# Values as the loaded operand of the value product in the second local-attention model

## The chip, the cores and the metric

The kernel runs on one core of one Trainium2 chip. The metric is the device time of one execution in microseconds (us). The engines of the core run side by side, each in the order of its own instruction list, and wait for each other through semaphores: TensorE (PE in the profile; its weight loads are shown apart as PEld), VectorE (DVE), ScalarE (ACT), GpSimd (POOL) and SyncE (SP), which here issues the DMAs.

## What is computed

Two blocks follow each other on a tensor of 2 sequences of 2048 tokens with 128 features. Each block is an adaptive layer norm around an attention part and a feed-forward part, and in each block the "feed-forward part" is itself a small transformer with local attention. The first of these (below: the first model) has 6 layers, 16 heads of 64 and windows of 32 tokens; the second has 2 layers, 8 heads of 64 and windows of 64 tokens. The change lies in the attention of the second one. For each head, each window of 64 queries looks at the 128 keys of its own window and the one before:

```
sim  = einsum('bhwid,bhwjd->bhwij', bq, bk)      # masked
attn = softmax(sim, -1)
out  = einsum('bhwij,bhwjd->bhwid', attn, bv)    # the value product
o    = out.transpose(0, 2, 1, 3).reshape(b, n, INNER)
x    = x + o @ wo
```

All of it is in float32.

## The kernel before, in words

The program has three stages. The first attention part takes a little over 600 us (the first value product of L1047 starts at 624 us). Then comes the first local model, and from about 4040 us to the end the second one. The linear attention that stands between the two models is cut in small steps ("lsteps") and woven in between the tiles of both.

A local model is worked off in tiles of 128 tokens. A layer has 16 tiles for each of the 2 sequences, so that the second model has 2 x 16 x 2 = 64 tiles. The main loop of `local_models` (L1484 on) writes several tiles in flight into one turn: the scores of tile i + 1, the projections of tile i + 3 (`project`), the values and the turning of queries and keys of tile i + 2 (`values`, `turn`), and the value product and output of tile i. A scheduling layer then settles the order on each engine, and puts one tile's work into the gaps of another's. The order in which the engines run is fixed when the program is built.

What a tile of the second model goes through, with its lines:

- `project` (L862): queries and keys from one matmul pair into PSUM (L871); squares on ACT (L873); rotary products on DVE (L881, L886); their sum on POOL (L892); norms on DVE (L897 and the small steps of `rsqrt_quick`, L167 to L180); the scaling on POOL (L904), whose result is the tile `r`.
- `turn` (L923): eight transposes of `r` on PE (L936) and two copies on ACT (L939, L941) give queries and keys with features on the partitions.
- `values` (L943): one matmul (L955), a copy on ACT (L956), and DMAs (L965 to L968) that lay out the 128 keys of each window on the partitions, in the tile `v2`, two tiles ahead of its use.
- `scores` (L974): the mask is written by a matmul (L986), and 16 matmuls of 64 x 64 x 128 add the scores (L995). Then come maximum (L1003) and difference (L1005) on DVE, the exponential on ACT (L1012), sum and reciprocal on DVE (L1019, L1020) and the scaling on POOL (L1021).
- `keys_first_` (L1023): eight transposes (L1030) and two copies on ACT (L1031) put the keys on the partitions, in the tile `pT`.
- `mix` (L1034): the value product. For each of 8 heads and 2 windows one matmul loads a 128 keys x 64 queries part of `pT` and streams the 128 keys x 64 features of `v2` through it (L1047), so that 64 queries lie on the partitions of the result. One copy on ACT (L1053) brings the PSUM bank to the tile `on`.
- `turn_out` (L1056): four transposes on PE (L1063) and a copy on ACT (L1064) turn `on` into `oT`, with features on the partitions.
- `project_out` (L1067): four matmuls with the output weights (L1075) and two additions on DVE (L1081).

Every fourth tile of a sequence a feed-forward step of that sequence's 512 tokens is queued (L1144 on) and worked off in the following turns; its hidden products are L1158, its Gelu on ACT L1168, its second product L1183. Exponential and Gelu need different tables on ACT, and each change between them costs an ACT_TABLE_LOAD, which the profile lists under the line of the activation that follows it.

PSUM banks for these steps come in turn from a pool of four (`bank`), so each new bank waits until the one four requests back has been read. `pT` and `oT` share one SBUF buffer; `on` has one of its own. `m.NO` is 128 / (2 x window): 2 in the first model, 1 in the second.

Of the kernel before, what the change touches and what calls it, by code (L numbers as in the profile page):

```python
# [72 lines left out]
def tile_kernel(ctx: ExitStack, tc: tile.TileContext, a: dict, out: bass.AP):  # L73
    nc = tc.nc
# [633 lines left out]
    def local_models(mA, mB, hs0):  # L708
# [12 lines left out]
        def bank(name):  # L721
            return psT.tile([128, 512], F32, tag="T", name=f"ps_{name}")
# [53 lines left out]
        st = [dict() for _ in range(n)]  # L776
# [4 lines left out]
        def load_proj(g, u):  # L781

            m, l = layers[g]
            w = wpool.tile([128, 1024], F32, tag="wp", name="wp", bufs=4)
            c = u * 1024
            k = min(1024, 3 * m.INNER - c)
            nc.sync.dma_start(w[:, 0:k], a[f"{m.pre}_ffn_Wqkv"][l, :, c:c + k])
            wts[g, u] = w

        def load_out(g):  # L790
            m, l = layers[g]
            w = wpool.tile([128, 8, 128], F32, tag="wo", name="wo", bufs=2)
            nc.sync.dma_start(
                w[:, 0:m.NPR, :], a[f"{m.pre}_ffn_Wo"][l].rearrange("(c p) m -> p c m", p=128)
            )
            wts[g, "o"] = w
# [41 lines left out]
        def factors(g):  # L838
            m, l = layers[g]
            f = wk.tile([128, 2, 2, DH], F32, name="fac", bufs=2)  # L840
            nc.vector.scalar_tensor_tensor(
                f[:, 0], m.sc, RSQ_C, m.qsc[:, :, l, :], ALU.mult, ALU.mult
            )
            for lo in (0, 32):
                nc.vector.tensor_copy(f[:, 1, :, lo:lo + 32], f[:, 0, :, 32 - lo:64 - lo])
            fac[g] = f
# [127 lines left out]
        def scores(i):  # L974

            g, b, t = tiles[i]
            m, _ = layers[g]
            W, H, HPG = m.W, m.H, m.HPG
            qT, kT = st[i].pop("q"), st[i].pop("k")
            sp = wide("s")  # L980
            for q in range(2):


                rows, sel, j = (slice(0, 128), identb, 0) if t == 0 else (
                    slice(64 * q, 64 * q + 64), pick, 1)
                nc.tensor.matmul(  # L986
                    sp[:, 512 * q:512 * q + 512], lhsT=sel[rows],
                    rhs=bc(m.maskb[rows, j].unsqueeze(1), (rows.stop - rows.start, HPG, 2 * W)),
                    start=True, stop=False,
                )  # L990
            for cc in range(HPG):
                for q in range(2):
                    for w in range(m.NW):
                        c0 = 512 * q + 2 * W * cc
                        nc.tensor.matmul(  # L995
                            sp[W * w:W * w + W, c0:c0 + 2 * W],
                            lhsT=qT[64 * q:64 * q + 64, cc, W * w:W * w + W],
                            rhs=kT[64 * q:64 * q + 64, cc, W * w:W * w + 2 * W],
                            start=False, stop=(cc == HPG - 1),
                        )  # L1000
            v = lambda x: x.rearrange("p (h k) -> p h k", k=2 * W)
            mx = wk.tile([128, 16], F32, name="mx")
            nc.vector.tensor_reduce(mx[:, 0:H], v(sp), AX.X, ALU.max)  # L1003
            sm = wk.tile([128, 1024], F32, name="sm", bufs=2)
            nc.vector.tensor_tensor(  # L1005
                v(sm), v(sp), bc(mx[:, 0:H].unsqueeze(2), (128, H, 2 * W)), ALU.subtract
            )
            st[i]["p"] = sm

        def weights_exp(i):  # L1010
            sm = st[i]["p"]
            nc.scalar.activation(sm, sm, AF.Exp)  # L1012

        def weights_norm(i):
            m, _ = layers[tiles[i][0]]
            sm = st[i]["p"]
            v = sm.rearrange("p (h k) -> p h k", k=2 * m.W)
            rs = wk.tile([128, 16], F32, name="rs", bufs=2)[:, 0:m.H]
            nc.vector.tensor_reduce(rs, v, AX.X, ALU.add)  # L1019
            nc.vector.reciprocal(rs, rs)  # L1020
            nc.gpsimd.tensor_tensor(v, v, bc(rs.unsqueeze(2), (128, m.H, 2 * m.W)), ALU.mult)  # L1021
# [12 lines left out]
        def mix(i):  # L1034

            m, _ = layers[tiles[i][0]]
            W, NO = m.W, m.NO
            pT, v2 = st[i].pop("pT"), st[i].pop("v")
            po = [bank("o") for _ in range(NO)]
            on = wk.tile([128, 2, 4, 128], F32, name="on")  # L1040
            for c in range(4):
                for s in range(NO):
                    kp = slice(2 * W * s, 2 * W * (s + 1))
                    for q in range(2):
                        co = 128 * c + 64 * q
                        for w in range(m.NW):
                            nc.tensor.matmul(  # L1047
                                po[s][W * w:W * w + W, co:co + 64],
                                lhsT=pT[kp, q, c, W * w:W * w + W],
                                rhs=v2[kp, w, co:co + 64], start=True, stop=True,  # L1050
                            )
            for s in range(NO):
                nc.scalar.copy(on[:, s].rearrange("p c i -> p (c i)"), po[s])  # L1053
            st[i]["on"] = on
# [34 lines left out]
        def step():  # L1089
            if steps:  # L1090
                steps.pop(0)()
# [4 lines left out]
        def lstep():  # L1096
            if lsteps:
                lsteps.pop(0)()
# [372 lines left out]
        for i in range(-3, n):  # L1471
            j = i + 3
            lstep()
            if 0 <= i + 1 < n:
                scores(i + 1)
                weights_exp(i + 1)
                weights_norm(i + 1)
            more = False
            if j < n:
                g, b, t = tiles[j]  # L1480
                jj = j % per
                nu = len(layers[g][0].units)
                more = g < last
                if g == second and t % 4 == 0:  # L1484
                    while (b, t // 4) not in ready:
                        lstep()
                if nu == 2:
                    project(j, 0)
                if more and jj == 4:
                    load_proj(g + 1, 0)  # L1490
                if more and jj == 6 and g + 1 == second:
                    models[1].consts()
                if jj == 6 and g == second - 1:
                    linear_consts()
                if more and jj == 8:
                    factors(g + 1)
                    if 2 == 2:
                        load_out(g + 1)
                if more and jj == 18:
                    load_ff(g + 1)  # L1500
                if more and jj == 22:
                    fold_ff(g + 1)
                if nu == 2 and more and jj == per - 1:
                    load_proj(g + 1, 1)
                lstep()
            step()
            if i >= 0:
                keys_first_(i)
            if 0 <= i + 2 < n:
                halo(i + 2)  # L1510
            if j < n:
                project(j, nu - 1)
                if nu == 2 and more and jj == per - 1 and g + 1 < second:
                    load_proj(g + 1, 2)
                if nu == 1 and more and jj == per - 1:
                    load_proj(g + 1, 1)
                if b == B - 1 and j + 1 < n:
                    tables(*tiles[j + 1][::2])
            lstep()
            if i >= 0:  # L1520
                mix(i)
            lstep()
            if 0 <= i + 2 < n:
                values(i + 2)
            lstep()
            if i >= 0:
                turn_out(i)
            if 0 <= i + 2 < n:
                for u in range(len(layers[tiles[i + 2][0]][0].units)):
                    turn(i + 2, u)  # L1530
            step()
            lstep()
            if i >= 0:
                g, b, t = tiles[i]
                project_out(i)
                if 2 == 1 and i % per == per - 1 and g < last:
                    load_out(g + 1)
                if t % 4 == 3:
                    feed_forward(g, b, t // 4)
# [9 lines left out]
    with ExitStack() as ctx2:  # L1549
        local_models(m0, m1, hs0)  # L1550
# [63 lines left out]
```

## Time and profile before

| | |
|---|---|
| median of 3 runs | 5001.14 us (4997.42 to 5006.03) |
| profiled execution, its own time | 5004.26 us |
| its span | 5002.5 us |
| mean granted TensorE clock | 0.961 of full |

Busy time in the stretch of the second model, 4043 us to the end (960 us), from the view of busy time by stretch:

| engine | busy us | share |
|---|---|---|
| PE | 846.9 | 88% |
| DVE | 721.8 | 75% |
| ACT | 544.1 | 57% |
| POOL | 442.1 | 46% |

A row of the groups view names the line, the engine and operation, the tiles written and read, shapes and count; then the busy time in us and the mean of one in ns; then the time for which the engine had stood idle just ahead of these instructions, and which work ended that. A matmul in float32 appears as two records, a transpose as one. The chain of waits is followed back from the last instruction: each piece has its start, the time it adds to the end, and the work. Matmul ends are modelled, so that four pipelined transposes show 0.66 us though their starts are only about 0.11 us apart.

### The profile page before, as it was taken

To read this page: it belongs to the slowest core of one execution; us is meant where nothing else is said; L and a number is where in the kernel's file an instruction comes from. 1 tells how busy PE (TensorE), PEld (TensorE's weight loads), DVE (VectorE), ACT (ScalarE), POOL (GpSimd) and SP (SyncE) were. 2 spreads that over 40 slices of the span, in tenths; PEclk is the share of its full clock that TensorE was granted. 3 is DMA by queue.
4 is the path that set the end of the run, shared out by engine and by line. 5 is a ranking of instruction groups with operands and counts; after the bars stand their busy time and mean duration, and the time that the engine had idled before them with its cause. 6 is when DMAs were issued, how large, how long until landed. Compare 5 with 4: busy or idle time off the path is not lost.

```text
span 5002.5 us, 170719 instructions
## 1 busy us (share of the span) xinstructions
PE 4572.7 (91%) x74820; PEld 3143.2 (63%) x74850; DVE 3973.1 (79%) x6840; ACT 2883.5 (58%) x4665; POOL 2780.8 (56%) x1666
## 2 busy tenths in 40 slices
PE   5667799999999999999999999999999989899897
PEld 4445566666666666666666666666666666555554
DVE  6993488888888888888888888888877777787885
ACT  3233366666666656666666666666555555565564
POOL 3332366666666666666666666666555544455452
PEclk8778899999999999999999999999999999999999
DMA  2000322222222322223222322232222211111111
GB/s 77 1 1 25 84 69 67 63 72 74 71 64 63 83 71 63 63 76 76 66 66 64 83 67 64 65 78 73 54 55 52 63 45 38 39 46 40 53 53 37
DMA packets 222487, 295.59 MB, mean 59 GB/s; under 512 B 75656, under 2 KB 95408, under 8 KB 221744
## 3 DMA queue, kind: packets, MB, share of 16 engines
q1 hardware_dynamic: 221744, 284.67, 22.0%
q8 instruction: 590, 9.67, 0.8%
q14 instruction: 153, 1.25, 0.1%
HBM read 40.98 MB, written 10.75 MB: 10 GB/s over the span
## 4 chain that ended last, share of the span: by engine, by line
PE 53%; DVE 20%; ACT 8%; POOL 5%; issue 3%; DMA 1%; SPq 0%; POOLq 0%; ACTq 0%; DVEq 0%
PE ps_qk L871 11%; PE ps_v L955 6%; PE ps_f L1158 5%; PE ps_turn L936 5%; PE ps_y L1075 5%; PE ps_o L1047 5%; PE ps_s L995 4%; DVE ps_qk L897 4%; POOL r L892 3%; DVE t L886 3%; PE ps_fy L1183 3%; PE ps_oT L1063 3%; ACT sq L873 2%; DVE r L881 2%; PE ps_pT L1030 2%
## 5 line engine op out<-in xcount | busy, mean ns | idle before, releaser
L892 POOL TENSOR_TENSOR r<-r,t 128x1024 f32<-128x1024 f32 x448 | 1061.2, 2369 | 995.9 <-DVE t L886 770.5
L904 POOL TENSOR_TENSOR r<-r,rq_y 128x1024 f32<-128x1024 f32 x448 | 844.0, 1902 | 455.9 <-DVE rq_y L180 439.2
L873 ACT ACTIVATE sq<-ps_qk 128x1024 f32<-128x1024 f32 x448 | 460.4, 1028 | 1006.4 <-PE ps_qk L871 999.9
L871 PE MATMUL ps_qk<-wp,hs 128*128 128x512 f32 x1792 | 884.4, 615 | 68.3 <-DVE rq_y L180 41.3
L881 DVE TENSOR_TENSOR r<-ps_qk,tb 128x1024 f32<-128x1024 f32 (+1 forms) x512 | 550.1, 1074 | 175.4 <-ACT sq L873 166.9
L886 DVE TENSOR_TENSOR t<-ps_qk,tb 128x1024 f32<-128x1024 f32 (+1 forms) x512 | 553.2, 1080 | 145.0 <-POOL r L892 144.5
L1021 POOL TENSOR_TENSOR sm<-sm,rs 128x1024 f32<-128x1024 f32 x256 | 487.2, 1903 | 263.3 <-DVE rs L1020 172.3
L897 DVE TENSOR_REDUCE ps_qk<-sq 128x16 f32<-128x1024 f32 x448 | 549.1, 1226 | 12.3
L1047 PEld LDWEIGHTS ps_o<-v,pT 64*32 64x32 f32 (+1 forms) x26624 | 356.8, 109 | 289.1 <-ACT pT L1031 175.7
L871 PEld LDWEIGHTS ps_qk<-wp,hs 128*128 128x128 f32 x1792 | 306.7, 191 | 326.2 <-issue 235.6
L955 PE MATMUL ps_v<-wp,hs 128*128 128x512 f32 x896 | 471.9, 639 | 1.0 <-ACT on L1053 0.6
L1047 PE MATMUL ps_o<-v,pT 64*32 64x64 f32 (+1 forms) x26624 | 418.1, 224 | 59.6 <-ACT pT L1031 32.7
L1075 PEld LDWEIGHTS ps_y<-oT,wo 128*128 128x128 f32 x3584 | 429.2, 192 | 48.0 <-issue 42.2
L936 PE MATMUL ps_turn<-ident,r 128*128 128x128 f32 x3584 | 443.2, 276 | 13.3 <-POOL r L904 11.8
L1075 PE MATMUL ps_y<-oT,wo 128*128 128x128 f32 x3584 | 446.3, 276 | 1.8 <-ACT oT L1064 1.8
L936 PEld LDWEIGHTS ps_turn<-ident,r 128*128 128x128 f32 x3584 | 405.7, 143 | 19.8 <-POOL r L904 16.6
L1003 DVE TENSOR_REDUCE mx<-ps_s 128x16 f32<-128x1024 f32 (+1 forms) x256 | 312.9, 1222 | 110.8 <-PE ps_s L995 107.4
L995 PE MATMUL ps_s<-kT,qT 64*32 64x64 f32 (+1 forms) x26624 | 371.6, 230 | 0.4
L1019 DVE TENSOR_REDUCE rs<-sm 128x16 f32<-128x1024 f32 (+1 forms) x256 | 310.3, 1212 | 68.6 <-ACT sm L1012 67.5
L1158 PE MATMUL ps_f<-fx,w 128*128 128x512 f32 (+1 forms) x768 | 356.4, 600 | 1.7 <-DVE fx L1141 1.7
L995 PEld LDWEIGHTS ps_s<-kT,qT 64*32 64x32 f32 (+1 forms) x26624 | 321.3, 107 | 57.1 <-issue 46.2
L956 ACT COPY vn<-ps_v 128x512 f32<-128x512 f32 x448 | 262.5, 586 | 112.3 <-PE ps_v L955 93.4
(268 smaller groups left out, 7554.6 us busy)
## 6 DMA issues: line engine op xcount, KB each, us to landing
v<-vn SPq DMA_DIRECT2D x1276, 128.0 KB
v<-vn SPq DMA_DIRECT2D x744, 64.0 KB
v<-vn SPq DMA_DIRECT2D x64, 256.0 KB
wp<-in_L_ffn_Wqkv SPq DMA_DIRECT2D x20, 512.0 KB
xD<-xb SPq DMA_DIRECT2D x24, 256.0 KB
xb<-xD SPq DMA_DIRECT2D x24, 256.0 KB
cs<-in_cos SPq DMA_DIRECT2D x128, 32.0 KB
cs<-in_sin SPq DMA_DIRECT2D x128, 32.0 KB
```

Of the source, the lines that this page charges most:

```text
L871: nc.tensor.matmul(pq[:, js], lhsT=hw, rhs=wts[g, u][:, js], start=True, stop=True)
L881: nc.vector.tensor_tensor(r[:, es].rearrange("p (h d) -> p h d", d=DH), pq[:, es].rearrange("p (h d) -> p h d", d=DH), bc(tb[:, 0, s].unsq ...
L886: nc.vector.tensor_tensor(t2[:, es].rearrange("p (h s d) -> p h s d", s=2, d=32), pq[:, es].rearrange("p (h s d) -> p h s d", s=2, d=32)[: ...
L892: nc.gpsimd.tensor_tensor(r, r, t2, ALU.add)
L897: nc.vector.tensor_reduce(pq[:, 16 * v:16 * v + 16], st[i].pop(("sq", v)).rearrange("p (h d) -> p h d", d=DH), AX.X, ALU.add,)
L904: nc.gpsimd.tensor_tensor(rv, rv, bc(y[:, 16 * v:16 * v + 16].unsqueeze(2), (128, 16, DH)), ALU.mult)
L936: nc.tensor.transpose(p[:, c * 128:(c + 1) * 128], r[:, cs], ident)
L955: nc.tensor.matmul(p, lhsT=hw, rhs=wv, start=True, stop=True)
L995: nc.tensor.matmul(sp[W * w:W * w + W, c0:c0 + 2 * W], lhsT=qT[64 * q:64 * q + 64, cc, W * w:W * w + W], rhs=kT[64 * q:64 * q + 64, cc, W ...
L1047: nc.tensor.matmul(po[s][W * w:W * w + W, co:co + 64], lhsT=pT[kp, q, c, W * w:W * w + W], rhs=v2[kp, w, co:co + 64], start=True, stop=True,)
L1075: nc.tensor.matmul(py[:, 0:128], lhsT=wts[g, "o"][:, c * NO + s, :], rhs=oT[:, s, c, :], start=(c + s == 0), stop=(c == 3 and s == NO - 1),)
L1158: nc.tensor.matmul(ps_[c][0:sz], lhsT=wts[g, "w1"][:, o:o + sz], rhs=S["x"], start=True, stop=True,)
```

## The change

In models with `NO == 1`, that is in the second one, the value product swaps its operands: the part of `v2` (128 keys x 64 features) is loaded and the part of `pT` (128 keys x 64 queries) is streamed. The result has the features of two heads on its 128 partitions and the queries along the free axis, as `oT` had. The copy on ACT brings it to `on`, and `project_out` reads `on` directly. `turn_out` isn't called for these tiles. The loop's innermost index is now the head of the pair (`q`), before it was the window (`w`). The first model keeps the old path.

```diff
             po = [bank("o") for _ in range(NO)]
             on = wk.tile([128, 2, 4, 128], F32, name="on")
+            if NO == 1:
+
+                for c in range(4):
+                    for w in range(m.NW):
+                        for q in range(2):
+                            co = 128 * c + 64 * q
+                            nc.tensor.matmul(
+                                po[0][64 * q:64 * q + 64, 128 * c + W * w:128 * c + W * w + W],
+                                lhsT=v2[:, w, co:co + 64], rhs=pT[:, q, c, W * w:W * w + W],
+                                start=True, stop=True,
+                            )
+                nc.scalar.copy(on[:, 0].rearrange("p c i -> p (c i)"), po[0])
+                st[i]["o"] = on
+                return
             for c in range(4):
                 for s in range(NO):
                     kp = slice(2 * W * s, 2 * W * (s + 1))
...
-            if i >= 0:
+            if i >= 0 and "on" in st[i]:
                 turn_out(i)
```

## Prediction

> **What bounds the kernel now.** I read the page's busy times and slices, then the busy time by stretch to find the second model, then groups and waits of that stretch (4043 us to the end), and last the chain of waits through it. On the page PE leads over the whole span:
>
> ```profile
> PE 4572.7 (91%) x74820; PEld 3143.2 (63%) x74850; DVE 3973.1 (79%) x6840; ACT 2883.5 (58%) x4665; POOL 2780.8 (56%) x1666
> ```
>
> The slices say that this holds for the first model (9 in each) but less for the last fifth, and only that part is changed. In it PE is busy 847 of 960 us, so 113 us are idle. The groups of that stretch, kept apart by form, and the waits of PE say where:
>
> ```profile
> L1047 PE MATMUL ps_o<-v,pT 128*64 128x64 f32 x2016 | 90.1, 236 | 23.2 <-ACT pT L1031 23.2
> L1063 PE MATMUL ps_oT<-ident,on 128*128 128x128 f32 x256 | 43.5, 295 | 27.8 <-ACT on L1053 27.3
> L1064 ACT COPY oT<-ps_oT 128x512 f32<-128x512 f32 x64 | 37.6, 588 | 39.5 <-PE ps_oT L1063 39.5
> PE ps_oT L1063 <- ACT on L1053: 27.3, 42, 2.0
> PE ps_turn L936 <- POOL r L904: 8.3, 8, 2.3
> ```
>
> The output transposes (L1063) are ahead of every other place in PE's waits: after the value product PE has to wait for ACT's copy before it can transpose. The chain shows that this is on the path, not only idle time. One tile near the end:
>
> ```profile
> 4889.90 1.72 PE ps_o L1047 x28
> 4891.62 0.02 issue
> 4891.64 0.59 ACT on L1053
> 4892.23 0.05 issue
> 4892.28 0.66 PE ps_oT L1063 x4
> 4892.94 0.87 PE ps_turn L936 x8
> 4893.81 2.58 PE ps_f L1158 x6
> 4896.39 0.90 PE ps_y L1075 x8
> ```
>
> The time between the value product and the turning of the next queries and keys is 0.02 + 0.59 + 0.05 + 0.66 = 1.32 us, in which PE does nothing but four transposes. The whole chain from 4040 us on runs through L1063 at 44 of the 64 tiles. But it is a mixed chain: between such places it goes over DVE (L1003, L1005), ACT (exponential and table loads) and POOL.
>
> **What is removed.** 64 tiles x 4 transposes on PE, 64 copies of 0.588 us on ACT (37.6 us), and PE's wait. From above, PE gets back at most busy plus wait, 43.5 + 27.8 = 71.3 us. That is too much for two reasons. Where PE had no wait, the transposes cost only the distance of their starts (about 0.44 us for four; 0.66 is the modelled end). And in some eight tiles the next work, the turn of L936, waits for POOL's r (8.3 us in all), so PE would only wait there instead.
>
> What is on the path I count on the chain: 44 steps of L1063 with 27.8 us, 36 steps of the copy to `on` (L1053) with 19.7 us, 6 of the copy to `oT` (L1064) with 3.5 us. That is **51 us**. The copy to `on` stays, but who waits for it changes: before, the transposes at once; after, the output product (L1075). PE does the turn first, 8 transposes of 0.87 us on the chain, against 0.05 + 0.59 us for the copy, so the new wait costs nothing where ACT is free. Where ACT is still at a square (1.02 us) when the product ends, the copy is late by that, and PE has the mask matmuls (L986, 2 x about 0.2) before the turn as well; I price it at nothing, at most 0.6 us in a tile. Without that cover the whole copy would be back on the path, 64 x 0.58 = 37 us. In the last two tiles there is no turn, and the copy stays visible; the transposes and their copy still go.
>
> **What is added.** Nothing in number: 16 matmuls before and after, each loading 128 x 64 and streaming 64 columns. The disputed price is that of the new form. The Trainium skill ("TensorEngine Tiling (Array Packing)", Performance Considerations) holds out up to twice the speed for swapping loaded and streamed operand together with column tiling where the streamed side is 64 or less. By that rule half of L1047's 90 us, 45 us, would come on top. The row says otherwise: the form before is 128*64 already, with an output of 64 partitions, so both halves of the array are taken before and after. I take the row: gain 0. The other bound is a loss. The output product streams 128 columns in about 0.13 us a record (8 in 1.05 us); 64 columns would be 0.065 us, yet 32 records of L1047 take 1.15 us in undisturbed tiles, 0.036 each. So two halves run side by side now. If they didn't after the swap, a product would cost 32 x 0.065 = 2.1 us, 0.95 more. Neighbouring matmuls still alternate between the halves (q inside, where it was w), so I take 0; the loss is kept for the rivals.
>
> The waits at the head of the product change places: `v2` is now loaded first, `pT` streamed. `v2` is written two tiles ahead, and no wait for its DMA shows among L1047's, so 0. The second matmul already needs the second copy of `pT`, before it was the third; the built order puts the values matmul (L955, about 1.05 us) in that gap as before, longer than the copy of 0.58. The `pT` buffer comes free earlier, since `oT` no longer sits in it, and `on` comes free at the output product, some 10 us before it is written again. A tile asks for one PSUM bank less, so each request looks back over other work; the banks it meets were read microseconds before. All these go at 0; a copy of 0.58 us in each tile (37 us) is the loss if I am wrong. SP's queue keeps its order but for five issues outside the attention.
>
> **What the scheduler moves.** The built order of the changed program has 148 table loads on ACT instead of 158: in five feed-forward steps the third Gelu now stands ahead of the exponential and not behind it. Each spares two loads:
>
> ```profile
> L1012 ACT ACT_TABLE_LOAD x26 | 33.4, 1283 | 39.9 <-DVE sm L1005 39.5
> L1168 ACT ACT_TABLE_LOAD x22 | 28.2, 1283 | 0.4
> ```
>
> The Trainium skill ("ScalarE: Activation LUTs", What ACT_TABLE_LOAD costs) states 1283 ns and about 1380 ns of drain, 2.66 us for a switch: ten would be 26.6 us. Here the chain has the exponential 0.01 us behind the load and the load 0.05 us behind its releaser; no drain is seen, so ten are 12.8 us of ACT. On the path I count less. In the chain at 4884 us an exponential ends at 4885.33, then load and Gelu follow, and the copy of `pT` that PE waits for starts at 4887.23: 1.9 us, of which the load is needed no more and the Gelu falls into ACT's earlier wait. 5 x 1.9 = **9.5 us**.
>
> **The sum.** 51 + 9.5 = 60 us from the path. Not all arrives: when PE is earlier, POOL's r and the copies of `pT` (23.2 us of PE's waits already) are late next, and DVE, busy 75% of the stretch, sets more of the pace. Much of that work starts from PE's own results (scores, projections) and moves up with it, so I take off a sixth: 50 us. The profiled execution, 5004.3 us (span 5002.5 and 1.8 around it), becomes 4954; the median lies 3.1 lower, so **4951 us**, 1.0% faster. A difference of 0.2% (10 us) is about what a measurement can tell.
>
> **Rivals.**
> 1. Likeliest (62%): as summed, 30 to 66 us less: 4935 to 4971.
> 2. The next wait takes half (20%): r (L904) and DVE's row of L1003, L1005, L1019 set the pace. For it: eight turns wait for r already, and the chain has long runs on DVE. Against it: DVE is idle a quarter of the stretch and its waits mostly end with PE or ACT. Gain 30 us or less: about 4973.
> 3. More than the path shows (11%): PE gets its 71 us nearly whole, as ACT also loses 37.6 + 12.8 = 50 us of work and the `pT` copies come earlier. For it: 23.2 us of waits for exactly these copies. Against it: the eight tiles bound by r. Gain 78 us: about 4923.
> 4. The swapped product is slower (4%): if the halves no longer overlap, 64 x 0.95 = 61 us are added at L1047, on the path behind which L1053 and L936 stand. Against the 50 us gained this gives 5012. It decides the sign from 0.8 us more a tile, that is, from about 1.95 us for an undisturbed product. Against it: same shape, same alternation.
> 5. It does nothing for the end (3%): the transposes were filler and DVE sets the pace throughout; 5001 within 10 us. Against it: 44 of 64 tiles on the chain.
>
> **How the numbers follow.** Faster by over 0.2% are cases 1 to 3, 0.93; within 0.2% is case 5, 0.03; slower is case 4, 0.04. The range leaves out the slow cases 4 and 5, the slower tail of case 2 and the far part of case 3: 4928 to 4977.
>
> **What would show it.** In the profile after, L1063 and L1064 keep only the first model's 1536 transposes and 384 copies. L1047's successor in the second model must stay near 90 us busy; over 120 would be case 4. The stretch of the second model should shrink from 960 to about 910 us with PE's share about unchanged or higher: 847 - 43.5 = 803 us of 910 is 88%. Waits of L936 for r should rise from 8.3, but stay under 25 us; well above that is case 2. Waits of L1075 for the copy to `on` should stay under 10 us. Table loads should count 148, and the first model's stretch should not change. I am wrong if the stretch shrinks by less than 30 us, or if the value product lengthens.

## The result: no change

The changed kernel takes 5001.44 us (median of 12 runs, 4997.21 to 5013.47), the kernel before in the same session 5001.52 us (12 runs, 4991.92 to 5008.41). The ratio is 0.9999, with a 95% interval of 0.9989 to 1.0008. The forecast was 4951 us. Its profiled execution took 5003.49 us, with a span of 5001.7 us, against 5004.26 and 5002.5 before; the mean granted TensorE clock was 0.956, against 0.961.

The swap did what the diff says. In the second model's stretch L1063 and L1064 are gone, the product still has 2016 recorded matmuls, and PE's wait for the copy to `on` has all but vanished. The groups of that stretch, by form (line and names; busy us and mean ns; idle before, and what ended it), after:

```profile
L1047 PE MATMUL ps_o<-pT,v 128*64 128x64 f32 x2016 | 93.4, 230 | 14.1 <-ACT pT L1031 14.0
L1172 PE MATMUL ps_f<-fx,w 128*128 128x512 f32 x144 | 81.5, 693 | 2.1 <-DVE fx L1155 1.8
L936 PE MATMUL ps_turn<-ident,r 128*128 128x128 f32 x496 | 75.7, 299 | 32.8 <-POOL r L904 32.8
```

And the waits of PE there, after (us in all, times, longest):

```profile
PE ps_turn L936 <- POOL r L904: 32.8, 11, 3.5
PE ps_o L1047 <- ACT pT L1031: 14.0, 33, 2.1
PE ps_out L1463 <- DVE xb L1219: 13.2, 4, 4.5
...
PE ps_y L1089 <- ACT on L1052: 1.5, 2, 0.7
```

The rows of before to set beside these (the value product, L1063 and two of the waits stand in the prediction):

```profile
L1158 PE MATMUL ps_f<-fx,w 128*128 128x512 f32 x144 | 72.8, 628 | 1.7 <-DVE fx L1141 1.7
L936 PE MATMUL ps_turn<-ident,r 128*128 128x128 f32 x496 | 69.6, 287 | 8.3 <-POOL r L904 8.3
PE ps_out L1449 <- DVE xb L1205: 4.7, 1, 4.7
```

The 27.3 us that PE waited for `on` are gone, and 9.2 us of its waits for `pT`. In their place the turn (L936) waits 32.8 us for POOL's `r`, where it waited 8.3, and the block output (now L1463) 13.2 us for DVE, where it waited 4.7. And some of PE's work got longer: the hidden products (L1158 before, L1172 now) had a mean of 628 ns and have 693, with the same shapes.

The sum of the busy times by stretch, 4043 us to the end, after:

```profile
sum 960.00, PE 837.68 PEld 536.20 DVE 714.49 ACT 498.53 POOL 443.64; mean PE 837.68 PEld 536.20 DVE 714.49 ACT 498.53 POOL 443.64
```

PE's busy time fell by only 9.2 us, from 846.9 to 837.7, and the stretch is 0.8 us shorter, so PE is idle 121 us in it and not 113. That gives an account of what PE was freed of. The row of L1063 says 43.5 us, but these records overlap with their neighbours: without them PE's busy time before would be 815.0 us, 31.9 less. With the waits for `on` and `pT` PE was thus freed of about 69 us. Of these 22.7 came back as longer times of the work that stayed (815.0 to 837.7), and 45 as new waits, over half of them for `r` (24.5).

The chain of waits shows how a tile comes to this. After, one tile in the middle of the stretch:

```profile
4702.42 0.18 DVE ps_qk L167
...
4702.63 1.23 DVE mx L1003
...
4703.97 1.23 DVE sm L1005
...
4705.30 1.06 ACT sm L1012
4706.36 0.02 issue
4706.38 1.22 DVE rs L1019
...
4708.01 0.17 POOL sm L1021
4708.18 1.69 issue
4709.87 1.91 POOL r L904
4711.78 0.04 issue
4711.82 1.28 PE ps_turn L936 x8
4713.10 4.08 PE ps_f L1172 x6
```

The norm's small steps (L167 to L180) run on DVE from 4702.42 to 4708.12, because one tile's maximum, difference and sum (L1003, L1005, L1019, about 1.2 us each) stand between the steps of another tile's norm. Then POOL scales that softmax first (L1021; the 0.17 and the 1.69 us of "issue" are its one instruction), and `r` after it, 1.6 us later than the norm would have let it start. PE stands still for 3.25 us ahead of the turn, so POOL's order is about half of this wait and DVE's the rest. The timeline of PE over the same place, after (start, length, work, and in brackets the wait ahead):

```profile
4711.82 1.28 PE L936 MATMUL ps_turn<-ident,r 128*128 128x128 f32 x8 [3.25 <-POOL r L904]
4712.90 4.29 PE L1172 MATMUL ps_f<-fx,w 128*128 128x512 f32 x6
...
4719.04 2.84 PE L1172 MATMUL ps_f<-fx,w 128*128 128x512 f32 x6
```

After a wait of 3.25 us, six hidden products take 4.29 us; six microseconds later the same six take 2.84 us. The trace's clock record has the half clock granted from 4712.6 to 4716.0. In the second model's stretch such windows sum to 76 us before and 115 us after, and PE is busy in 68.5 and 103.5 us of them.

`r` is not late everywhere. Before, it was ready more than 1.2 us ahead of the turn in 55 of the 64 tiles, by 6.8 us in the median; after, in 41 tiles, by 2.7 us in the median. PE's waits for it return in a pattern of eight tiles: before in tiles 25, 33, 41 and 30, 38, 46, 54, 62 (tiles counted from 0), after in these and in 22, 49 and 57. Measured from the end of one tile's value product to the next, the two traces show where the time goes. In the six steps with the turns of tiles 22, 30, 38, 46, 54 and 62 the changed kernel loses 4.1 to 8.1 us each on the kernel before, 32.5 us in all: from tile 44 to 45, say, it takes 19.3 us where 15.3 were taken before, with a wait for `r` of 3.25 us where 0.3 was. In three more (to tiles 43, 51 and 59) it waits 2.9 us for the block output's input from DVE and loses 4.7 us each. In the rest it gains, and from the first product to the last the gain is -0.2 us.

What took the removed steps' place on the chain of waits, from 4043 us on, is the whole row that leads to `r`. The projection (L871) is on it with 59.5 us and not 25.6, the rotary products on DVE (L881, L886) with 67.1 and not 30.3, the norm's sum (L897) with 33.1 and not 22.9; the scaling (L904) itself grows from 17.1 to 20.9.

### The profile page after: what moved, and what is told of

Its sections match the earlier page's. It is cut to its first block, busy times and chain, and to the rows that moved or that the text cites. A ratio compares the mean times of both kernels' runs of the same rounds, so it can differ in the third digit from the quotient of the medians.

```text
span 5001.7 us, 170087 instructions
## 1 busy us (share of the span) xinstructions
PE 4561.0 (91%) x74564; PEld 3129.5 (63%) x74594; DVE 3968.7 (79%) x6840; ACT 2842.1 (57%) x4591; POOL 2784.7 (56%) x1666
## 4 chain that ended last, share of the span: by engine, by line
PE 54%; DVE 20%; ACT 7%; POOL 5%; issue 3%; DMA 0%; SPq 0%; POOLq 0%; DVEq 0%; ACTq 0%
PE ps_qk L871 12%; PE ps_v L955 6%; PE ps_turn L936 5%; PE ps_f L1172 5%; PE ps_y L1089 5%; PE ps_s L995 4%; PE ps_o L1061 4%; DVE ps_qk L897 4%; DVE t L886 4%; POOL r L892 3%; PE ps_fy L1197 3%; DVE r L881 2%; ACT sq L873 2%; PE ps_oT L1077 2%; DVE rs L1019 2%
## 5 line engine op out<-in xcount | busy, mean ns | idle before, releaser
L892 POOL TENSOR_TENSOR r<-r,t 128x1024 f32<-128x1024 f32 x448 | 1063.6, 2374 | 1003.8 <-DVE t L886 789.1
L904 POOL TENSOR_TENSOR r<-r,rq_y 128x1024 f32<-128x1024 f32 x448 | 844.6, 1903 | 444.8 <-DVE rq_y L180 428.9
L871 PE MATMUL ps_qk<-wp,hs 128*128 128x512 f32 x1792 | 884.5, 615 | 75.8 <-DVE rq_y L180 44.0
L881 DVE TENSOR_TENSOR r<-ps_qk,tb 128x1024 f32<-128x1024 f32 (+1 forms) x512 | 550.5, 1075 | 172.3 <-ACT sq L873 164.3
L886 DVE TENSOR_TENSOR t<-ps_qk,tb 128x1024 f32<-128x1024 f32 (+1 forms) x512 | 554.5, 1083 | 148.2 <-POOL r L892 147.6
L1021 POOL TENSOR_TENSOR sm<-sm,rs 128x1024 f32<-128x1024 f32 x256 | 487.8, 1906 | 253.4 <-DVE rs L1020 158.8
L897 DVE TENSOR_REDUCE ps_qk<-sq 128x16 f32<-128x1024 f32 x448 | 549.1, 1226 | 12.0
L871 PEld LDWEIGHTS ps_qk<-wp,hs 128*128 128x128 f32 x1792 | 307.3, 191 | 333.5 <-issue 239.0
L936 PE MATMUL ps_turn<-ident,r 128*128 128x128 f32 x3584 | 449.7, 278 | 39.3 <-POOL r L904 36.3
L955 PE MATMUL ps_v<-wp,hs 128*128 128x512 f32 x896 | 468.9, 636 | 1.3 <-ACT on L1052 0.8
L936 PEld LDWEIGHTS ps_turn<-ident,r 128*128 128x128 f32 x3584 | 406.6, 143 | 59.3 <-POOL r L904 43.2
L1061 PEld LDWEIGHTS ps_o<-v,pT 64*32 64x32 f32 x24576 | 282.0, 106 | 194.5 <-ACT pT L1031 139.6
L1003 DVE TENSOR_REDUCE mx<-ps_s 128x16 f32<-128x1024 f32 (+1 forms) x256 | 313.2, 1224 | 111.5 <-PE ps_s L995 107.9
L1089 PEld LDWEIGHTS ps_y<-oT,wo 128*128 128x128 f32 x3072 | 363.5, 192 | 33.4 <-issue 32.2
L1089 PE MATMUL ps_y<-oT,wo 128*128 128x128 f32 x3072 | 375.0, 275 | 0.1
L1172 PE MATMUL ps_f<-fx,w 128*128 128x512 f32 (+1 forms) x768 | 364.7, 612 | 2.1 <-DVE fx L1155 1.8
L1019 DVE TENSOR_REDUCE rs<-sm 128x16 f32<-128x1024 f32 (+1 forms) x256 | 310.5, 1213 | 61.4 <-ACT sm L1012 60.0
L1061 PE MATMUL ps_o<-v,pT 64*32 64x64 f32 x24576 | 327.4, 223 | 32.0 <-issue 21.3
L1031 ACT COPY pT<-ps_pT 128x512 f32<-128x512 f32 x512 | 273.9, 585 | 101.5 <-PE ps_pT L1030 101.2
```

What stands on the lines that cost most here:

```text
L871: nc.tensor.matmul(pq[:, js], lhsT=hw, rhs=wts[g, u][:, js], start=True, stop=True)
L881: nc.vector.tensor_tensor(r[:, es].rearrange("p (h d) -> p h d", d=DH), pq[:, es].rearrange("p (h d) -> p h d", d=DH), bc(tb[:, 0, s].unsq ...
L886: nc.vector.tensor_tensor(t2[:, es].rearrange("p (h s d) -> p h s d", s=2, d=32), pq[:, es].rearrange("p (h s d) -> p h s d", s=2, d=32)[: ...
L892: nc.gpsimd.tensor_tensor(r, r, t2, ALU.add)
L897: nc.vector.tensor_reduce(pq[:, 16 * v:16 * v + 16], st[i].pop(("sq", v)).rearrange("p (h d) -> p h d", d=DH), AX.X, ALU.add,)
L904: nc.gpsimd.tensor_tensor(rv, rv, bc(y[:, 16 * v:16 * v + 16].unsqueeze(2), (128, 16, DH)), ALU.mult)
```

## Experiments

The forecast's view was that PE's path carries the stage, so that the saving arrives whatever PE meets next. The expectations use letters for the theories of where it went:

- A: the time saved on PE became a wait for `r`. In A1 `r` is late by the built order on POOL; in A2 by DVE's norm steps, with POOL's order as a side effect; A3 says that the granted clock is what stays lost once `r` is early.
- B: DVE's work in its order sets the pace, whatever PE saves.
- C: the longer waits bring the half clock, and so give the time back.
- D: the order built for the changed program is worse.
- E: the swapped product saves nothing by itself.

On POOL's order the traces show this: in 12 tiles of the second model the softmax scaling (L1021) stands between the sum (L892) and the scaling (L904) of `r`; before, in 3. In 10 of the 11 waits of the turn for `r` after (30.9 of the us), L1021 is what POOL had just finished when it began `r`. Before, the same holds for 3 of the 8 waits (6.8 of the 8.3 us).

Most experiments are pairs: the same edit in the kernel before and in the changed one, so that the difference of the two is what the swap is worth under that edit. Edits act on the second model only, and are shown as made to the changed kernel; they shift line numbers by a few. What stands ahead of the second model isn't touched; still its first value product starts anywhere from 4028 to 4056 us in the traces, so a difference of a few us between two runs says nothing.

### PE gets its four transposes back

```diff
+        def fill(i):
+            pT = st[i].pop("fill")
+            p = bank("fill")
+            for c in range(4):
+                nc.tensor.transpose(p[:, c * 128:(c + 1) * 128], pT[:, 0, c, :], ident)
...
+            elif i >= 0:
+                fill(i)
```

The four results are read by nobody; `fill` stands where `turn_out` stood.

> The changed kernel, with four transposes of pT put back on TensorE where the output transposes stood; nothing copies or reads their result. Theory A (the time saved on TensorE became a wait for POOL's r at L936): the transposes fill that wait, 5001 us within 10, and the wait for r falls from 33 us back towards 10. Theory B (VectorE's in-order work sets the pace): also within 10 us of 5001. Theory C (the longer gaps cost granted clock: half-clock windows rose from 77 to 116 us in the second model's stretch): filling the gaps gives the clock back, 10 to 25 us faster than both kernels. Theory D (the order that the scheduler made for the changed program is worse, since here the order and the 158 table loads of before come back): 20 to 40 us faster than both.

Measured: 5003.88 us, ratio to the kernel before 0.9989 (0.9977 to 1.0001). So the wait for `on` and the copies to `oT` are gone here, the transposes are not, and that too brings next to nothing. Theory D, which had 20 to 40 us, is out; of theory C's 10 to 25 us some 5 came (12 at most), though the half-clock windows fell from 115 to 84 us. Four transposes a tile are some 28 us of PE (64 x 0.44, an estimate from the distance of their starts in the trace), and PE takes them in without a longer stage: its waits for `r` fall from 32.8 to 23.0 us, though those for `pT` rise from 14.0 to 21.7. The changed kernel itself was not measured beside this one. The edit also brings the table loads back to 158, and L1021 stands ahead of L904 in 9 tiles, not 12, so it isn't a pure test.

### `r` is not scaled

```diff
-                for v in range(len(units)):
+                for v in range(len(units) if m.NO > 1 else 0):
```

The scaling of `r` (L904) is left out in the second model in both kernels, so that `r` is ready 1.9 us earlier and POOL has 64 x 1.9 = 122 us less to do.

> The kernel before without the scaling of r on POOL (L904) in the second model, so queries and keys stay unscaled there; r is ready 1.9 us after its sum. Theory A: PE waited only 8 us for r before, so little is won, 0 to 15 us (4986 to 5001). Theory B: 0 to 5 us.

> The changed kernel, also without the scaling of r on POOL in the second model. Theory A: with r earlier the saving of the swap comes through, 25 us or more below the same cut of the kernel before (about 4960). Theory B: within 10 us of that kernel. Theory D (worse order): within 10 us of it as well.

Measured: 4983.91 us for the kernel before (0.9952, 0.9936 to 0.9969), 4932.96 us for the changed one (0.9852, 0.9832 to 0.9872). The pair differs by 51 us. The kernel before gains some 24 us by the edit, where 15 were expected at most and the trace has 8.3 us of waits for `r`: so leaving the scaling out helps in more ways than by ending these waits. The waits of PE, changed kernel with this edit:

```profile
PE ps_o L1047 <- ACT pT L1031: 12.5, 31, 2.1
PE ps_r L1152 <- POOL frt L1134: 11.5, 4, 4.3
PE ps_out L1463 <- DVE xb L1219: 11.2, 4, 4.6
```

There is no wait for `r` in them. In the kernel before with the edit the wait for `on` is still there (29.6 us). So once `r` is early a saving of the forecast's size comes through. Its parts are not those of the forecast, though: half-clock windows are 76 us in the kernel before with this edit and 43 us in the changed one, and PE is busy in 68.3 and 37.3 us of them. At half speed that is up to 15.5 us of the 51, which the forecast hadn't counted (an estimate from the two traces).

### The softmax without its maximum

```diff
+            if m.NO == 1:
+                st[i]["sp"] = sp
+                return
...
-            nc.scalar.activation(sm, sm, AF.Exp)
+            nc.scalar.activation(sm, st[i].pop("sp", sm), AF.Exp)
```

The maximum and the difference (L1003, L1005) are left out, and the exponential reads the scores; 64 x 2.44 = 156 us of DVE work go.

> The kernel before without the maximum and the difference in the second model's softmax (L1003, L1005 left out, the exponential reads the scores in PSUM): 64 x 2.44 = 156 us less work on VectorE. Theory A1: some gain, since the weights come sooner, but TensorE's work and its wait for the copy to on stay: 20 to 80 us faster. Theory B (VectorE sets the pace): 100 us faster or more.

> The changed kernel without the maximum and the difference. The built order has r ahead of the softmax scaling in every tile, as in the same cut of the kernel before. Theory A1: the swap gives its 40 to 60 us against that kernel, since nothing stands ahead of r. Theory B: 40 us or more too, as VectorE no longer sets the pace. Theory E (the swapped product saves nothing by itself): within 10 us of that kernel.

Measured: 4887.8 us (0.9769, 0.9749 to 0.9789) and 4856.0 us (0.971, 0.9686 to 0.9734); the pair differs by 32 us, less than either theory had. With 2.44 us less on DVE in each tile the kernel before gains 113 us, as theory B said and more than the swap was ever to bring, and its waits for `on` shrink to 3.1 us. PE is then busy nearly all the time. The two traces have the same half-clock windows in the stretch (20 and 19 us) and the same number of table loads, so this pair shows the swap most by itself: it is worth what its transposes take of a busy PE, 64 x 0.44 = 28 us, and a little more. L1021 is ahead of L904 in no tile of the kernel before and in 2 of the changed one, where the expectation had none.

### `r` first on POOL

```diff
-            nc.gpsimd.tensor_tensor(v, v, bc(rs.unsqueeze(2), (128, m.H, 2 * m.W)), ALU.mult)
+            with tc.issue_after(last904[0].ins) if m.NO == 1 else nullcontext():
+                nc.gpsimd.tensor_tensor(v, v, bc(rs.unsqueeze(2), (128, m.H, 2 * m.W)), ALU.mult)
```

`last904` holds the newest scaling of `r`; the softmax scaling is queued behind it on POOL.

> The kernel before with one order fixed on POOL in the second model: the scaling of r (L904 of the kernel before) is queued ahead of the next scaling of the softmax weights (L1021). In the kernel before, that holds already for all but 3 tiles. Theory A1 (POOL's built order puts the softmax scaling ahead of r): three waits of 2.3 us go, 0 to 12 us faster (4989 to 5001). Theory B (VectorE sets the pace): no change.

> The changed kernel with the same order fixed on POOL; in the changed kernel 12 tiles had the softmax scaling ahead of r. Theory A1: ten of the eleven waits for r shrink by the 1.9 us of the softmax scaling, and the half-clock windows that follow them go too: the wait of the turn for r falls from 33 us to 15 or less, and the time to between 4955 and 4975. Theory A2 (r is late because VectorE's norms are late, POOL's order is a side effect): 10 us or less faster, 4990 to 5001. Theory B: no change.

Measured: 4995.33 us (0.9988, 0.9981 to 0.9995) and 4977.66 us (0.9958, 0.9946 to 0.997): the swap is worth 18 us here. Of the changed kernel's waits the one for `r` falls from 32.8 to

```profile
PE ps_turn L937 <- POOL r L905: 18.3, 11, 1.9
```

The 14.5 us that went are the time for which `r`'s finished norm had stood behind L1021 in the ten waits. POOL's order is thus a part of the loss and not all of it. In 10 of the 11 waits left POOL is free, and starts `r` 0.14 us after DVE's last norm step. How much time the order is worth is less sure than the 18 us: in the two traces the second model, from its first value product to the end, takes 950 us before and 943 changed, 7 us less, and the traced execution of the changed kernel is the slowest of its 13 (4997.68 us).

### `r` first on POOL, and the norm steps asked ahead on DVE

```diff
+                with tc.high_priority(200) if m.NO == 1 else nullcontext():
                     y = rsqrt_quick([pq[:, k * 32:k * 32 + 2 * H] for k in range(4)], 2 * H, wk)
```

Added to the edit above, around the norm steps and the scaling.

> The kernel before with the same two orders. There the turn waits for r only 3 us in all once POOL's order is fixed, so theory A says within 8 us of the 4995 us of that run; then the swap's own saving, from this kernel to the one beside it, is 30 us or more. Theory B: the same small change in both, and the saving stays at 18 us.

> The changed kernel with r hurried on two engines in the second model: VectorE's norm steps (L167 to L180) get a higher priority in the scheduler, so that they stand ahead of the softmax sum, and POOL scales r ahead of the softmax weights as in the run before. Theory A (r is what is late, by POOL's order and by VectorE's): the wait of the turn for r falls from 18 us to under 8, and the time from 4978 to between 4950 and 4968. Rival A3 (what remains is granted clock, not r): the wait for r falls, but the time stays within 8 us of 4978. Theory B (VectorE as a whole sets the pace, order does not matter): within 8 us of 4978, and other waits for VectorE rise by what r's falls.

Measured: 4994.95 us (0.9986, 0.9976 to 0.9996) and 4980.75 us (0.996, 0.9944 to 0.9976), as without the priority; the two intervals touch, and the waits for `r` are 18.1 us, where under 8 were expected. The priority left DVE's order in the late tiles as it was, with maximum, difference and sum still between the norm steps, so the run says nothing on what an earlier norm would bring.

### A fixed order on both engines

```diff
+            with tc.issue_after(lastrq[0].ins) if m.NO == 1 else nullcontext():
                 nc.vector.tensor_reduce(mx[:, 0:H], v(sp), AX.X, ALU.max)
```

Added to "`r` first on POOL": `lastrq` is the newest last norm step (L180), so the maximum of the next softmax is queued behind it on DVE.

> The kernel before with the same two fixed orders. r was hardly waited for there, so nothing is to be won: 4985 to 5005 by theory A and A3. Theory B: 5000 to 5020, since the softmax comes later.

> The changed kernel with r first on both engines, now as a fixed order: in the second model VectorE finishes the norm steps (to L180) before it takes the next scores' maximum (L1003), and POOL scales r ahead of the softmax weights. In the run with a higher priority the steps still stood between the maximum, the difference and the sum (three of 1.2 us), and r came as late as before. Theory A (r is what is late): the turn's wait for r falls from 18 us to under 8, time 4950 to 4968. Theory B (VectorE's row is full in these stretches, whatever its order): r's wait falls, but the softmax comes later and TensorE waits for pT instead; 4970 to 4990. Theory A3 (the rest is granted clock): r's wait falls and the time stays at 4972 to 4982.

Measured: 4973.13 us for the kernel before (0.9942, 0.9922 to 0.9962), faster than was expected of it, and 4963.04 us for the changed one (0.993, 0.9907 to 0.9952). The order helps both kernels; the swap is worth 10 us in medians, and the two intervals overlap. The changed kernel's time is what theory A had for it (4950 to 4968). The waits of PE, changed kernel with this order:

```profile
PE ps_pT L1034 <- POOL sm L1025: 14.0, 11, 2.3
PE ps_out L1467 <- DVE xb L1223: 11.6, 4, 4.6
...
PE ps_f L1176 <- DVE fx L1159: 8.6, 7, 1.4
```

No wait for `r` over 0.5 us is left, but the key transposes now wait for the softmax scaling, as theory B had it. POOL is not what holds that scaling up. The longest of these waits, from the timelines of POOL and PE:

```profile
4615.69 1.90 POOL L906 TENSOR_TENSOR r<-r,rq_y 128x1024 f32<-128x1024 f32 x1
4621.81 1.90 POOL L1025 TENSOR_TENSOR sm<-sm,rs 128x1024 f32<-128x1024 f32 x1 [4.23 <-DVE rs L1023]
4623.76 1.97 PE L1034 MATMUL ps_pT<-ident,sm 128*128 128x128 f32 x8 [2.28 <-POOL sm L1025]
```

POOL had finished `r` and stood idle for 4.23 us, until DVE had the softmax's sum and its reciprocal. In 10 of the 11 waits POOL was idle for over 2.7 us ahead of the scaling and began it within 0.2 us of the reciprocal. So it is on DVE that the two compete: whichever of the norm and the softmax goes first there, the other is late.

### The softmax scaling on ACT

```diff
-            nc.gpsimd.tensor_tensor(v, v, bc(rs.unsqueeze(2), (128, m.H, 2 * m.W)), ALU.mult)
+            for h in range(m.H):
+                nc.scalar.mul(v[:, h], v[:, h], rs[:, h:h + 1])
```

This leaves POOL to `r`: eight activations on ACT for each tile. The first run makes this edit alone, in the changed kernel.

> The changed kernel with the softmax scaling moved from POOL to ScalarE in the second model, eight activations by head with a scale per partition, so that nothing stands ahead of r on POOL. ScalarE has lost 50 us of copies and table loads in the changed kernel, and gets 64 x 8 x about 0.25 us = 130 us. Theory A: the wait for r falls to 20 us or less, as with POOL's order fixed; if ScalarE has room, 4960 to 4980, and if its longer row delays the copies that TensorE waits for, 4990 to 5030.

Measured: 4976.7 us (0.9958, 0.9946 to 0.9971). The waits for `r` sum to 1.5 us; instead PE waits for ACT, 15.9 us for `pT` with one of 4.9 us, and 10.7 us for `on`.

The second pair adds DVE's order of the section above (the maximum behind the norm steps).

> The kernel before, second model only: VectorE finishes the norm steps of r before the next tile's maximum (L1003), and the softmax scaling (L1021) leaves GpSimd for ScalarE as eight activations of one head each, so that r's scaling (L904) has nothing ahead of it. If the two scalings' contest for GpSimd is what eats the swap's saving, r and the scaled softmax are both early here; the kernel before still waits for the copy `on` (L1053, over 25 us) and takes 4960 to 4985 us. If ScalarE becomes the bound, it is slower than 4990 us, with longer waits for pT.

> The same two edits on the changed kernel. If the contest of r and of the softmax scaling for GpSimd is the cause, both waits (for r at the turn, for the scaled softmax at the transposes of pT) are gone together and the swap's saving comes through again: 30 us or more below the run of the kernel before with the same edits, about 4945 us. If VectorE's own row of steps sets the pace whatever GpSimd does, the pair differs by 15 us or less and this run stays near 4963, with the waits for VectorE (xb at L1463, fx at L1172) and for pT grown. If ScalarE is full, waits for pT and for the copy `on` grow.

Measured: 5038.12 us for the kernel before (1.007, 1.0055 to 1.0084), and 4953.66 us for the changed one (0.9898, 0.9882 to 0.9914). The waits of PE, kernel before with both edits:

```profile
PE ps_oT L1070 <- ACT on L1060: 54.4, 30, 3.2
PE ps_y L1082 <- ACT oT L1071: 14.6, 9, 2.0
PE ps_o L1054 <- ACT pT L1038: 10.0, 12, 3.9
```

And of the changed kernel with both:

```profile
PE ps_r L1159 <- POOL frt L1141: 12.5, 4, 4.3
PE ps_out L1470 <- DVE xb L1226: 11.4, 4, 4.5
...
PE ps_o L1054 <- ACT pT L1038: 7.8, 10, 3.9
```

The changed kernel waits neither for `r` nor for the softmax scaling here, and it is 49.7 us faster than the kernel before without edits. That this is the size that was forecast for the swap alone is chance, since two further edits are in it. DVE does the same work as ever, so DVE's busy time as such was not the limit; the order in which `r` and the softmax were finished, and what stood behind them, was. Why the wait for the softmax scaling is gone isn't settled: POOL was free for it in the run above, but here the scaling comes in eight pieces, and in the tile at 4620 us the first key transposes start at 4622.31, ahead of the end of the last piece at 4622.66.

The pair's difference of 84 us is more than the swap's own value, since it is made on a loaded ACT: the scaling is 152 us of work there (0.31 us a piece, where 0.25 was expected), and in the kernel before the copies to `on` and `oT` come late behind it (69 us of waits, against 29 without the edits). The expectation for the kernel before had named longer waits for `pT` for that case; it was these two copies. Of the kernels that leave nothing out this one is the fastest, 1.0% under the kernel before. "A fixed order on both engines", without ACT, reaches 0.7%.

What the swap is worth, in medians, and the half-clock windows from 4043 us on in the one traced execution of each kernel (us):

| edit in both kernels | before | changed | difference | half clock before | half clock changed |
|---|---|---|---|---|---|
| none | 5001.5 | 5001.4 | 0 | 76 | 115 |
| `r` not scaled | 4983.9 | 4933.0 | 51 | 76 | 43 |
| no maximum | 4887.8 | 4856.0 | 32 | 20 | 19 |
| `r` first on POOL | 4995.3 | 4977.7 | 18 | 53 | 95 |
| the same, with priority on DVE | 4995.0 | 4980.8 | 14 | 50 | 92 |
| fixed order on DVE and POOL | 4973.1 | 4963.0 | 10 | 46 | 69 |
| DVE's order, softmax scaling on ACT | 5038.1 | 4953.7 | 84 | 95 | 57 |

The two go together: the swap is worth 32 us in the pair with the same half clock on both sides, less where the changed kernel has more of it, and more where it has less. That doesn't say which of waits and clock is the cause.

## Why the prediction was wrong

**What held.** The removal itself is worth its time where the next results are early: 32 us with the clock alike on both sides, 51 us with `r` early and the half clock shorter. That the second figure is the forecast's 50 is in part luck. The product in its new form costs what the old one did. With PE nearly always busy (the pair without a maximum) its 2048 records sum to 75.7 us, 0.0370 us each, against 74.8 us, 0.0365, in the kernel before; so neither the gain by the rule of the Trainium skill ("TensorEngine Tiling (Array Packing)", Performance Considerations) nor the loss of case 4 came, and the row was right. PE's wait for `on` at the output product is 1.5 us, under the bound of 10. Table loads count 148; what these ten fewer bring by themselves no run isolates.

**What failed: "so I take off a sixth".** The step rested on the sentence that "Much of that work starts from PE's own results (scores, projections) and moves up with it". It doesn't move up. `r` comes out of some twelve microseconds of DVE and POOL work (4699.5 to 4711.8 us in the tile above), in a row that these two work off in their own order, with softmax steps in between; PE earlier by a microsecond finds the same `r` at the same time. The deduction should have been all of the 60 us and was 10. The eight waits of 8.3 us that the prediction saw at L936 were no odd tiles: they are the late tiles of a pattern of eight, and since each engine keeps its order, most of what the tiles between gain is given up there. The waits grew to 32.8 us in the same eight places and three more. Rival 2 named this mechanism and gave it half the gain. The forecast's own sign ("well above that is case 2", for more than 25 us of waits for `r`) reads 32.8, and the stretch shrank by 0.8 us where under 30 was to mean wrong. Case 5 has the number, 5001, but not the mechanism: DVE's amount of work does not set the pace throughout, or the fixed orders and the scaling on ACT, which leave it as it is, could not give 35 to 50 us.

**What was mis-sized: busy time.** The prediction took the whole 43.5 us of L1063 off PE's busy time (to 803 us); in the trace the transposes are 31.9 us of it.

**What was not priced: the built order on POOL.** The prediction compared the built orders on ACT (table loads) and on SP, and said of what the scheduler moves nothing for POOL. There L1021 came ahead of L904 in 12 tiles, before in 3, and makes `r` late by up to 1.8 us there. Undoing it takes 14.5 of the 32.8 us of waits away, and brings 18 us in the pair's medians (7 in the traces).

**What was not priced: the granted clock.** Longer waits for `r` (3.5 us the longest, before 2.3) come with more half clock: nine of the eleven end within 1.6 us of the start of a half-clock window. PE is busy in 35 us more of such windows (103.5 and not 68.5); at half speed that is 17.5 us of time, an estimate from the two traces, and most of the 22.7 us by which PE's remaining work got longer. Over the runs of one kernel the time goes down by 1.5 to 4 us for each 0.001 of mean clock (12 to 32 runs, correlation -0.56 to -0.93). No run held the clock while the waits stayed, so that the waits brought the half clock is argued, not shown.

**What stays open.** The parts overlap. The new waits, the norm steps that stand between softmax steps on DVE, POOL's order and the clock each have a number above, but no experiment takes one away and leaves the rest, and the edit that brings `r` in time (no scaling) also takes 122 us of work from POOL. A split of the lost 50 us was not reached.

## What to carry to other kernels

When work leaves an engine that waits often, look for the result that arrives next-latest at each of its waits, how early it was, and in what pattern of tiles. `r` was early by 6.8 us in the median tile; that it was late in two tiles of every eight was enough, for on engines that keep their order the late tile takes what the others gain. Two rows of steps that share in-order engines (here the norm and the softmax on DVE and on POOL) need an order, or separate engines, before a saving elsewhere can come through: the same swap was worth 0, 10, 14, 18, 32, 51 or 84 us by what happened there. And compare the built order on every engine that feeds the freed one, not only on those the change touches.

## What the runs showed of the hardware

- A single wait of PE of 3.25 us was followed by 3.4 us of half clock, in which six hidden products took 4.29 us and not 2.84. The Trainium skill ("TensorE: Matmul & The Clock Gate", Part 1: The HAM clock gate) has the half rate after an idle window of about 3.4 us. Here shorter waits came with it too: before the change, five waits of 2.5 us for `pT` (at L1047) were each followed within about 1 us by a half-clock window. Not every such wait is: one of 3.19 us for `r` was not. The windows in the second model's stretch, 76 to 115 us of 960, could cost up to 4 to 6% of it (half their length, an estimate).
- With the change, the engine that it relieved took longer for some of the same work: the hidden products went from 628 to 693 ns in the mean, the turn from 287 to 299 ns; the values products (L955) did not (666 and 654 ns).
- One scaling of 128 x 1024 takes 1.90 us on POOL as one instruction; as eight activations on ACT it takes 2.46 us in one tile of the trace, with a mean of 394 ns for each record.
